# Moving the softmax sums of four heads behind one head's values, and the next rope in front of their reciprocal

## The chip, the cores and the metric

The kernel runs on one core of one Trainium2 chip. The core has a matrix engine (TensorE; in profiles PE for its products and PEld for the loading of the stationary operand), a vector engine (VectorE, DVE), a scalar engine (ScalarE, ACT), a general engine (GpSimd, POOL) and a queue engine (SyncE, SP) that issues most DMA transfers. Each engine works through its own instructions in order, and waits on semaphores for the others. Products land in PSUM, which is used here as eight banks of 128 x 512 float32; everything else is in SBUF. All data is float32, and PE carries out each float32 product as two products in the trace.

The metric is the time of one execution in microseconds of device time. The kernel before takes 1343.32 us (median of 10 runs, 1342.91 to 1344.06).

## The reference, cut to what matters

One transformer block in parallel form: `x + attention(layernorm(x)) + experts(layernorm(x))`, with 4 sequences of 512 tokens and 512 features. The part that the change touches is the attention with 16 heads:

```python
q = concatenate([q_C, rope(q_R)]); k = concatenate([k_C, rope(k_R)])   # 128 + 64 per head
scores = clip(q @ k.T, -80, 80);  scores = where(causal, scores, -inf)
weights = softmax(scores / sqrt(192))
out = (weights @ v).reshape(B, S, H * D_H) @ W_O.T
```

The softmax is computed without a maximum: the exponentials `pt` are multiplied with the values first, and the result of each head is divided by the sums of its exponentials later.

## The kernel before, in words

The first half of the program (to about 655 us) is layernorm, routing and the experts, with pieces of attention's preparation mixed in. The second half is attention, in a loop (L1678 on) over `n` = 32 pairs of heads (4 sequences x 8 pairs), `i` = 0 to 31. Two pairs make a group `q` of four heads. The groups share one row-sum product, one reciprocal, one division and one output projection.

Nearly every instruction is wrapped in `keep(...)`, which pins it to the order in which the Python code names it. So the order of calls in the loop is the order of each engine's queue. For one pair `i` it is:

1. `scores(i)`: PE makes the scores of both heads, transposed, into six PSUM banks: `a0`, `a1` (first key block of each head), `b0`, `b1` (second and fourth block), `c` (third block of the first head) and `sd_i` (third block of the second head). The last one is not a bank of its own but one from the pool `ps_p`, tag `pj`, which has three buffers and hands them out in turn.
2. `rotary_query(i + 1)` and `query(i + 1, 0)`: PE makes the rotary part `pqr` and the first head's query `pq_0` of the next pair, each into a `pj` buffer.
3. `weights(i)`: DVE clips the six banks into `pt_i` in the order `a0`, `a1`, `sd`, `c`, `b0`, `b1` (line 1457), ACT takes exponentials (L1461), POOL multiplies the diagonal blocks with a triangle (L1465) and then adds the four key blocks of each head into a 128 x 512 tile `su_i_j` (L1489 and L1493). The rope of the next pair's query, `turn_q`, is five DVE products (L1266 and L1269) and a POOL subtraction (L1270). On odd `i` it stands right behind the clips on DVE and in front of the `su` additions on POOL; on even `i` it is named after the sums, and so stands behind the reciprocal on DVE and behind the `su` additions on POOL.
4. On even `i` from 2 on: `sums(q)` with `q = i // 2 - 1`. PE adds the 128 partitions of four tiles `su` (those of pairs `i-2` and `i-1`) with a 128 x 32 block of ones, four products that fill the four 32-partition strips of one tile `sb` in bank `a0` (L1528). DVE takes the reciprocal `rc` (L1530). `spread_by_dma` issues 16 DMAs on SP that copy each strip of `rc` four times into a tile `rb` of 128 partitions (L1540).
5. `values(i - 1, 0)`: PE multiplies `pt` of the last pair's first head with the values, four products into a `pj` buffer `av` (L1509); ACT copies it to `og` (L1519).
6. `query(i + 1, 1)`, then on some pairs preparation for the next sequence, then `values(i - 1, 1)`.
7. On even `i` from 4 on `project_out(q - 1)`: the output projection of the group before, 56 products of 128 x 256 in PE's records, with DVE and POOL additions into `acc`. On odd `i` from 3 on `divide(q)`: DVE multiplies the four heads in `og` with `rb` (L1560) and forms factors for the projection (L1566, L1569).

So the three `pj` buffers are taken, in one pair of the steady loop, by `sd`, `pqr`, `pq_0`, `av_0`, `pq_1`, `av_1`, in that order: `av_0` follows `sd` in its buffer, and may be written only when DVE has clipped `sd`. In the same way `sb` may be written only when DVE has clipped bank `a0`, and the next pair's scores may be written into `a0` only when DVE has read `sb` for the reciprocal. There are 15 groups whose sums run in the loop (`i` = 2, 4, ... 30); the last group's stand after it.

Of the kernel before, what the change touches and what calls it, by code (L numbers as in the profile page):

```python
# [42 lines left out]
def kernel(  # L43
# [1166 lines left out]
    def lat(b, i):  # L1210
        return xnT[:, i, ts(b, S)]
# [40 lines left out]
    def turn_keys(b, psum=None):  # L1252
        if psum is None:
            dst, src = (lat(b, i).rearrange("p (k f) -> p k f", k=TPB) for i in (3, 1))
            for step in turn4(dst, src):
                step()
            return
        tp = psum(f"ckvt_{b}")
        for k in range(TPB):
            keep(nc.tensor.transpose(tp[:, ts(k, P)], lat(b, 1)[:, ts(k, P)], ident))  # L1260
        keep(nc.scalar.copy(lat(b, 3), tp))
# [16 lines left out]
    def rotary_query(i, ps):  # L1278
        b, hp = pairs[i]
        keep(nc.tensor.matmul(ps, qrT[:, hp, :], lat(b, 0), start=True, stop=True))  # L1280
        raw = hw.tile([P, S], F32, tag="raw", name=f"qraw_{i}")
        qr = hw.tile([P, S], F32, tag="qr", name=f"qr_{i}", bufs=1)
        qs[i] = [qr]

        def copy():
            keep(nc.scalar.copy(raw, ps))

        def turn():
            rope(qr, raw, f"q{i}")

        return copy, turn

    def query(i, j, ps):
        b, hp = pairs[i]
        keep(nc.tensor.matmul(ps, a_h[:, 2 * hp + j, :], lat(b, 0), start=True, stop=True))  # L1295
        qc = hw.tile([P, S], F32, tag=f"qc{j}", name=f"qc_{i}_{j}", bufs=1)
        qs[i].append(qc)

        def copy():
            keep(nc.scalar.copy(qc, ps))  # L1300

        return copy
# [99 lines left out]
    def psum(name):  # L1402
        return ps_p.tile([P, S], F32, tag="pj", name=name)
# [6 lines left out]
    def scores(i):  # L1410
        b = pairs[i][0]
        qr, *qc = qs.pop(i)
        bank = {}
        for j in range(2):
            bank[j, 0] = ps_s.tile([P, S], F32, tag=f"a{j}", name=f"sa_{i}_{j}")
            bank[j, 1] = bank[j, 3] = ps_s.tile([P, S], F32, tag=f"b{j}", name=f"sb_{i}_{j}")
        bank[0, 2] = ps_s.tile([P, S], F32, tag="c", name=f"sc_{i}")
        bank[1, 2] = psum(f"sd_{i}")

        def where(j, kc):  # L1420
            o = 3 * P if kc == 3 else 0
            return bank[j, kc][:, o : o + PT_W[kc]]

        order = [(j, kc) for kc in (0, 2, 1, 3) for j in range(2)]
        for j, kc in order:

            keep(
                nc.tensor.matmul(  # L1428
                    where(j, kc),
                    lat(b, 1)[:, ts(kc, P)],  # L1430
                    qc[j][:, kc * P :],
                    start=(kc != 3),
                    stop=False,
                )
            )
        for j, kc in order:
            r = slice(j * DHR, (j + 1) * DHR)
            keep(
                nc.tensor.matmul(  # L1439
                    where(j, kc),  # L1440
                    lat(b, 2)[r, ts(kc, P)],
                    qr[r, kc * P :],
                    start=False,
                    stop=(kc != 1),
                )
            )
        return bank

    def weights(i, bank, then, behind):

        pt = ap.tile([P, 5 * S], F32, tag="pt", name=f"pt_{i}")

        def clip(to, src):
            keep(nc.vector.tensor_scalar(to, src, CLIP, -CLIP, ALU.min, ALU.max))  # L1457

        def exp(t):

            keep(nc.scalar.activation(t, t, AF.Exp, scale=QK_SCALE))  # L1461

        def mask(t, at, k=1, step=P):
            m = t[:, at : at + P]
            keep(nc.gpsimd.tensor_mul(m, m, tri))  # L1465

        for j in range(2):
            a = pt[:, ts(j, S)]
            clip(a, bank[j, 0])
            exp(a)  # L1470
            mask(pt, PT[j, 0])
        half = 2 * P
        for j in (1, 0):
            clip(pt[:, PT[j, 2] : PT[j, 2] + half], bank[j, 2][:, :half])
        exp(pt[:, ts(2, S)])
        for j in range(2):
            mask(pt, PT[j, 2])
        then()
        for j in range(2):
            t = pt[:, ts(3 + j, S)]  # L1480
            clip(t, bank[j, 1])
            exp(t)
            mask(pt, PT[j, 1])
            mask(pt, PT[j, 3])
        behind()
        su = []
        for j in range(2):
            t = ap.tile([P, S], F32, tag="su", name=f"su_{i}_{j}", bufs=4)
            keep(nc.gpsimd.tensor_copy(t[:, :P], pt[:, PT[j, 0] : PT[j, 0] + P]))  # L1489
            for kc in range(1, TPB):  # L1490
                prev = pt[:, PT[j, 0] + P : PT[j, 0] + S] if kc == 1 else t[:, kc * P :]
                keep(
                    nc.gpsimd.tensor_add(  # L1493
                        t[:, kc * P :], prev, pt[:, PT[j, kc] : PT[j, kc] + PT_W[kc]]
                    )
                )
            su.append(t)
        pts[i], sus[i] = pt, su
# [3 lines left out]
    def values(i, j):  # L1502

        b, q = pairs[i][0], i // 2
        pt = pts[i]
        av = psum(f"av_{i}_{j}")
        for kc in range(TPB):
            keep(
                nc.tensor.matmul(  # L1509
                    av[:, kc * P :],  # L1510
                    lat(b, 3)[:, ts(kc, P)],
                    pt[:, PT[j, kc] : PT[j, kc] + PT_W[kc]],
                    start=(kc == 0),
                    stop=(kc == TPB - 1),
                )
            )
        if q not in og:
            og[q] = ap.tile([P, 4, S], F32, tag="og", name=f"og_{q}")
        keep(nc.scalar.copy(og[q][:, 2 * (i % 2) + j, :], av))  # L1519

    def bank(tag):
        return lambda name: ps_s.tile([P, S], F32, tag=tag, name=name)

    def sums(q):

        sb = bank("a0")(f"sb_{q}")
        for j, su in enumerate(sus.pop(2 * q) + sus.pop(2 * q + 1)):
            keep(nc.tensor.matmul(sb[ts(j, 32), :], ones[:, :32], su, start=True, stop=True))  # L1528
        rc = ap.tile([P, S], F32, tag="rc", name=f"rc_{q}", bufs=1)
        keep(nc.vector.reciprocal(rc, sb))  # L1530
        return rc
# [3 lines left out]
    def spread_by_dma(q, rc):  # L1535
        spread[q] = []
        for j in range(4):
            rb = ap.tile([P, S], F32, tag="rb", name=f"rb_{q}_{j}", bufs=4)
            for m in range(4):
                nc.sync.dma_start(rb[ts(m, 32), :], rc[ts(j, 32), :])  # L1540
            spread[q].append(rb)
# [123 lines left out]
    def combine(g):  # L1665
        for k, yg in enumerate(picks.pop(g)):
            keep(
                nc.vector.scalar_tensor_tensor(  # L1668
                    acc[:, g, :], yg, wk[:, g, k : k + 1], acc[:, g, :], ALU.mult, ALU.add
                )  # L1670
            )
# [6 lines left out]
    for i in range(n):  # L1678
        more = i + 1 < n
        even = i % 2 == 0  # L1680
        q = i // 2 - 1
        held = scores(i)
        raw_copy, turn_q = rotary_query(i + 1, psum(f"pqr_{i + 1}")) if more else (nothing, nothing)
        qc_copy = query(i + 1, 0, psum(f"pq_{i + 1}_0")) if more else nothing
        weights(i, held, raw_copy, nothing if even else turn_q)
        qc_copy()
        if even and i > 0:
            spread_by_dma(q, sums(q))
        if even:
            turn_q()  # L1690
        if i > 0:
            values(i - 1, 0)
        if more:
            query(i + 1, 1, psum(f"pq_{i + 1}_1"))()
        if i < 2:
            project(2 + i, psum)
        if 1 < i < 5:
            turn_keys((2, 3, 1)[i - 2], psum)
        if i > 0:
            values(i - 1, 1)  # L1700
        if even and i > 2:
            project_out(q - 1, first_added=lambda: combine(q))
        if i == 1:
            combine(0)
        if even and i != 2 or i == 1:
            fetch((i + 1) // 2)
        if not even and i > 1:
            divide(q)

    q = n // 2 - 1  # L1710
# [60 lines left out]
```

## Time and profile before

| What | Value |
|---|---|
| median of 10 runs | 1343.32 us |
| the profiled execution: its own time | 1343.4 us |
| its span, from first to last instruction | 1341.6 us |
| granted TensorE clock, mean | 0.999 |
| PE products busy | 1329.7 us (99%) |
| DVE busy | 967.3 us (72%) |
| POOL busy | 851.6 us (63%) |
| ACT busy | 406.0 us (30%) |
| DMA queue 1 | 34.0% of 16 engines |

The page gives each engine's busy time over the whole span. A row of the timeline has a start and a length in us, then the engine, the line, the operation, what it writes and reads, the shape and how many instructions were merged into the row; in brackets stands how long the engine had been idle before it and what ended that. "issue" means that nothing in the profile ended it. PE's products are pipelined: a row's start is firm, its end is modelled, and the time that a product occupies PE is read from the distance of starts. Over the 32 pairs a group of two pairs takes about 41.3 us (the first weights of `sb` of two neighbouring groups start at 860.09 and 901.38).

### The profile page before, as it was taken

The numbers are of one execution on the slowest core, as the hardware profiler recorded it, in microseconds if no ns is written. First come the engines' busy times: TensorE is split into PE (matmuls) and PEld (weight loads), VectorE is DVE, ScalarE is ACT, GpSimd is POOL, SyncE is SP. The second block draws the span as 40 slices with busy tenths as digits, with TensorE's granted clock in tenths as the row PEclk, the third lists the DMA queues.
The fourth block names the chain that finished last, engine by engine and source line by source line (L and its number), as shares of the span: only waits on it lengthen the run. The fifth ranks groups of instructions, "written<-read, shape, count | busy, mean of one in ns | idle before, by whom it ended". The sixth has DMA issues, their size and how long they took to land.

```text
span 1341.6 us, 17908 instructions
## 1 busy us (share of the span) xinstructions
PE 1329.7 (99%) x5949; PEld 993.1 (74%) x5949; DVE 967.3 (72%) x1414; ACT 406.0 (30%) x714; POOL 851.6 (63%) x956
## 2 busy tenths in 40 slices
PE   9999999999999999999999999999999999999997
PEld 8778888888888888877655766666666666666675
DVE  7669486666766676676458678877789777798774
ACT  3333222322223322222224333332323323243231
POOL 5113664554545465532267889888898888888883
PEclk9999999999999999999999999999999999999999
DMA  7850356766667675522401331243321333313342
GB/s 276 193 160 20 92 133 159 220 187 175 196 166 199 170 218 162 169 86 92 152 21 36 110 110 53 74 125 110 110 81 55 117 110 110 105 35 121 102 121 76
DMA packets 174101, 167.90 MB, mean 125 GB/s; under 512 B 57905, under 2 KB 136753, under 8 KB 174001
## 3 DMA queue, kind: packets, MB, share of 16 engines
q1 hardware_dynamic: 161264, 133.10, 34.0%
q0 software_dynamic: 12736, 33.57, 8.5%
q8 instruction: 49, 0.80, 0.2%
q14 instruction: 52, 0.42, 0.1%
HBM read 116.02 MB, written 34.87 MB: 112 GB/s over the span
## 4 chain that ended last, share of the span: by engine, by line
PE 98%; DVE 1%; ACT 0%; issue 0%; POOL 0%; DVEq 0%; ACTq 0%; POOLq 0%
PE op L228 14%; PE hr L228 11%; PE yr L228 11%; PE av L1509 11%; PE gr L228 10%; PE sb L1428 4%; PE sa L1428 4%; PE pq L1295 4%; PE gs L228 3%; PE sa L1439 3%; PE ys L228 2%; PE pqr L1280 2%; PE hs L228 2%; PE sb L1439 2%; PE sb L1528 2%; PE h_s L142 1%
## 5 line engine op out<-in xcount | busy, mean ns | idle before, releaser
L180 POOL DMA_INDIRECT xs<-xn_d,idx_i x208 | 229.0, 1101 | 195.0 <-DVE xT L197 136.0
L1465 POOL TENSOR_TENSOR pt<-pt,tri 128x128 f32<-128x128 f32 x256 | 139.6, 566 | 69.1 <-ACT pt L1461 62.3
L1461 ACT ACTIVATE pt<-pt 128x512 f32<-128x512 f32 x160 | 94.4, 628 | 258.1 <-DVE pt L1457 257.1
L1509 PEld LDWEIGHTS av<-pt,xnT 128*128 128x128 f32 x512 | 95.4, 190 | 83.7 <-issue 47.7
L1509 PE MATMUL av<-pt,xnT 128*128 128x512 f32 (+3 forms) x512 | 149.8, 436 | 0.0
L228 PE MATMUL op<-m,og 128*128 128x256 f32 x512 | 118.8, 380 | 0.8 <-DVE og L1560 0.8
L1269 DVE TENSOR_TENSOR swap_q<-qraw,sinT 32x512 f32<-32x512 f32 x128 | 117.7, 919 | 1.7
L1493 POOL TENSOR_TENSOR su<-su,pt 128x256 f32<-128x256 f32 (+1 forms) x128 | 105.2, 822 | 10.0
L228 PEld LDWEIGHTS op<-m,og 128*128 128x128 f32 x512 | 95.9, 190 | 15.0 <-DVE og L1560 1.9
L1457 DVE TENSOR_SCALAR pt<-sa 128x512 f32<-128x512 f32 x64 | 41.0, 682 | 75.2 <-PE sa L1439 75.2
L1603 POOL TENSOR_TENSOR acc<-acc,v 128x512 f32<-128x512 f32 x64 | 85.6, 1339 | 14.4 <-DVE acc L1606 8.5
L1655 POOL DMA_INDIRECT yg<-y_d,pos_i x48 | 54.5, 1135 | 56.6 <-issue 50.0
L228 PE MATMUL op<-m,s 128*128 128x256 f32 x384 | 88.1, 379 | 0.0
L1493 POOL TENSOR_TENSOR su<-pt 128x384 f32<-128x384 f32 x64 | 83.8, 1310 | 0.0
L228 PEld LDWEIGHTS op<-m,s 128*128 128x128 f32 x384 | 73.0, 190 | 9.9
L1606 DVE TENSOR_TENSOR acc<-op,acc 128x512 f32<-128x512 f32 x48 | 31.7, 686 | 54.9 <-POOL acc L1603 47.3
L1668 DVE SCALAR_TENSOR_TENSOR acc<-yg,wk,acc 128x512 f32<-128x512 f32 x48 | 56.7, 1181 | 19.1 <-POOL acc L1603 17.9
L1599 ACT COPY v<-op 128x512 f32<-128x512 f32 x64 | 37.5, 585 | 108.4 <-PE op L228 107.2
L1560 DVE TENSOR_TENSOR og<-og,rb 128x512 f32<-128x512 f32 x64 | 68.2, 1126 | 0.6 <-PE rb L1548 0.2
L228 PE MATMUL yr<-w,at_r 128*128 128x256 f32 x288 | 66.9, 380 | 0.3
L228 PE MATMUL hr<-xT,w 128*128 128x256 f32 x288 | 66.1, 379 | 0.0
L228 PE MATMUL gr<-xT,w 128*128 128x256 f32 x288 | 66.1, 379 | 0.0
(337 smaller groups left out, 2805.3 us busy)
## 6 DMA issues: line engine op xcount, KB each, us to landing
m<-m_d SPq DMA_DIRECT2D x112, 256.0 KB, 5.7
w<-in_L_ffn_W_dram SPq DMA_DIRECT2D x52, 512.0 KB, 4.4
rb<-rc SPq DMA_DIRECT2D x240, 64.0 KB, 2.0
w<-in_L_ffn_Wg_dram SPq DMA_DIRECT2D x26, 512.0 KB, 3.5
y_d<-v_yr SPq DMA_DIRECT2D x36, 256.0 KB, 2.2
y_d<-none SPq DMA_DIRECT2D x24, 256.0 KB, 4.7
acc<-in_L_attn_x_dram SPq DMA_DIRECT2D x16, 256.0 KB, 4.7
xn_d<-xp SPq DMA_DIRECT2D x16, 256.0 KB, 2.4
```

The costliest lines, as they stand in the source:

```text
L180: nc.gpsimd.indirect_dma_start(out=xs[blk][:, q, :], out_offset=None, in_=xn_d[:, :], in_offset=bass.IndirectOffsetOnAxis(ap=idx_i[:, q, b ...
L228: nc.tensor.matmul(banks[k][:, t, :], a[p][:, j, ts(t, P)], b[p][:, j, :], start=(k not in used), stop=(t == j == 1), skip_group_check=True,)
L1269: keep(nc.vector.tensor_mul(swap[there, :], raw[here, :], tables[1][here, :]))
L1428: nc.tensor.matmul(where(j, kc), lat(b, 1)[:, ts(kc, P)], qc[j][:, kc * P :], start=(kc != 3), stop=False,)
L1439: nc.tensor.matmul(where(j, kc), lat(b, 2)[r, ts(kc, P)], qr[r, kc * P :], start=False, stop=(kc != 1),)
L1461: keep(nc.scalar.activation(t, t, AF.Exp, scale=QK_SCALE))
L1465: keep(nc.gpsimd.tensor_mul(m, m, tri))
L1493: nc.gpsimd.tensor_add(t[:, kc * P :], prev, pt[:, PT[j, kc] : PT[j, kc] + PT_W[kc]])
L1509: nc.tensor.matmul(av[:, kc * P :], lat(b, 3)[:, ts(kc, P)], pt[:, PT[j, kc] : PT[j, kc] + PT_W[kc]], start=(kc == 0), stop=(kc == TPB - 1),)
L1560: keep(nc.vector.tensor_mul(o[:, j, :], o[:, j, :], rb))
L1603: keep(nc.gpsimd.tensor_add(block, block, v))
L1668: nc.vector.scalar_tensor_tensor(acc[:, g, :], yg, wk[:, g, k : k + 1], acc[:, g, :], ALU.mult, ALU.add)
```

## The change

In the loop over pairs, the block `if even and i > 0: spread_by_dma(q, sums(q))` moves down by two statements: behind `turn_q()` and behind `values(i - 1, 0)`.

```diff
         weights(i, held, raw_copy, nothing if even else turn_q)
         qc_copy()
-        if even and i > 0:
-            spread_by_dma(q, sums(q))
         if even:
             turn_q()
         if i > 0:
             values(i - 1, 0)
+        if even and i > 0:
+            spread_by_dma(q, sums(q))
         if more:
             query(i + 1, 1, psum(f"pq_{i + 1}_1"))()
```

On PE the four products of `sb` then stand behind the four of `av_0` and in front of `pq_1`. On DVE the reciprocal stands behind the five products of the rope instead of in front of them. On SP the 16 DMAs of `rb` keep their place between the same neighbours. ACT and POOL keep their orders. No instruction is added or left out.

## The prediction

> **What bounds the kernel now.** I read the page's busy times first, then the chain that ended last, then the waits of the attention half, then two even pairs instruction by instruction.
>
> ```profile
> PE 1329.7 (99%) x5949; PEld 993.1 (74%) x5949; DVE 967.3 (72%) x1414; ACT 406.0 (30%) x714; POOL 851.6 (63%) x956
> ...
> PE 98%; DVE 1%; ACT 0%; issue 0%; POOL 0%; DVEq 0%; ACTq 0%; POOLq 0%
> ```
>
> PE is the bound: its chain is 98% of the span. A change pays or costs what it does to PE's stream, and idle DVE or POOL time is worth nothing by itself. A modelled 99% hides short stops, so I looked at what the weight loads waited for:
>
> ```profile
> PEld av L1509 <- DVE pt L1457: 15.3, 29, 0.8
> ...
> PEld sb L1528 <- DVE pt L1457: 11.4, 15, 0.8
> ...
> PEld sb L1528 <- POOL su L1493: 4.4, 13, 0.4
> ```
>
> (Total us, times, longest.) In 13 of the 15 groups PE stops inside the sums for POOL's last `su` addition. And the first `av` product of a pair is released by a clip of DVE. Now the typical group `q` = 5, even pair `i` = 12, first PE's weight loads, then DVE, then POOL:
>
> ```profile
> 900.44 0.19 PEld L1295 LDWEIGHTS pq<-xnT,a_h 128*128 128x128 f32 x1 [0.24 <-issue]
> 901.38 0.15 PEld L1528 LDWEIGHTS sb<-su,ones 128*32 128x32 f32 x6 [0.76 <-DVE pt L1457]
> 901.88 0.14 PEld L1528 LDWEIGHTS sb<-su,ones 128*32 128x32 f32 x2 [0.34 <-POOL su L1493]
> 902.85 0.30 PEld L1509 LDWEIGHTS av<-pt,xnT 128*128 128x128 f32 x2 [0.84 <-DVE pt L1457]
> ```
>
> ```profile
> 899.22 1.48 DVE L1569 TENSOR_TENSOR og<-og 128x512 f32<-128x512 f32 x1
> 900.63 1.28 DVE L1457 TENSOR_SCALAR pt<-sa 128x512 f32<-128x512 f32 x2
> 901.83 0.41 DVE L1457 TENSOR_SCALAR pt<-sd 128x256 f32<-128x256 f32 x1
> 902.16 0.41 DVE L1457 TENSOR_SCALAR pt<-sc 128x256 f32<-128x256 f32 x1
> 902.49 1.27 DVE L1457 TENSOR_SCALAR pt<-sb 128x512 f32<-128x512 f32 x2
> 903.68 3.34 DVE L1530 RECIPROCAL rc<-sb 128x512 f32<-128x512 f32 x1
> 906.95 0.80 DVE L1266 TENSOR_TENSOR qr<-qraw,cosT 128x512 f32<-128x512 f32 x1
> 907.76 4.08 DVE L1269 TENSOR_TENSOR swap_q<-qraw,sinT 32x512 f32<-32x512 f32 x4
> ```
>
> ```profile
> 900.23 1.59 POOL L1493 TENSOR_TENSOR su<-su,pt 128x256 f32<-128x256 f32 x2
> ```
>
> `pq_0` starts at 900.43 and gives PE free at 901.29 (two products, 0.43 apart). `sb`'s weights go in at 901.38, but those of the second pair's `su` only at 901.88, 0.06 after POOL's addition ends at 901.82. DVE comes late out of the last odd pair's `divide`: it starts the clips only at 900.63, ends `a0` at about 901.30 and `sd` at 902.24. Today the clip of `sd` hides behind `sb`.
>
> **The change part by part.**
>
> *The wait for `su`, removed.* By the chain, `sb` takes 1.47 us and `av_0` 2.35 here, 3.82 together. At `q` = 0, where `su` was long ready, they take 1.00 + 2.35 = 3.35. So the wait is worth 0.47 a group. After the change `sb` starts over 2 us later than `su` ends, so it's gone: 13 x 0.47 = 6.1 us gained, if nothing takes its place.
>
> *The new neighbours of `sb`.* `sb` uses a quarter of the array's columns at a time, and PE stops in front of and behind it: weights at 901.38 instead of at the product before, and `av` takes 2.35 behind `sb` against 2.16 behind `pq`. After the change the stops stand between `av` and `sb` and between `sb` and `pq`. The trace has such a pair of edges in the last group: two `av` take 4.31 (2 x 2.16), then `sb` 0.99 by the chain, and its 0.1 behind `sb` falls on the projection. So I keep 3.35 for both blocks in either order, cost 0, bounds -0.1 to +0.1 a group.
>
> *The new wait: `av_0` for the clip of `sd`.* `av_0` takes over `sd`'s `pj` buffer, the fourth of three buffers in turn, so its first weights wait for that clip. Without a wait they go in one product ahead: on an odd pair `pq` ends at 846.16 and the weights of `av` go in at 845.73. Now they go in at 902.24 + 0.06 = 902.30, and the product holds PE 0.1 longer since its load hides behind nothing (902.86 to the next `pq` at 905.12 is 2.26, against 846.16 to 848.32). The stop is 902.30 + 0.10 - 901.29 = 1.11 us. The block then takes 3.35 + 1.11 = 4.46 instead of 3.82: **+0.64 us a group**. The other groups from `q` = 2 on have the same distances within 0.02, with one sum: where DVE is 0.1 later (`q` = 4), `su` is too. Group 1 has no `su` wait: `pq_0` is over at 736.13, the clip of `sd` ends at 736.62, so the stop is 736.68 + 0.10 - 736.13 = 0.65, less 0.02 that `sb` loses today: +0.63. Group 0 has DVE early (clip of `sd` over at 705.14, `pq_0` at 706.54): 0. Sum: 13 x 0.64 + 0.63 = 8.9, say **+8.9 us**. This already contains the gain above.
>
> Behind the waiting weight load stand all of PE's later products, so `sb`, `pq_1`, `av_1` and the projection move with it. Nobody makes it up: DVE's clips on odd pairs wait for PE (4.04 us idle at 884.51), so DVE's lateness starts anew from PE's scores each group, and its 16 us of unbroken work to the next even clip stay as they are.
>
> *The rope ahead of the reciprocal on DVE.* Its copy `qraw` is there in time (ACT, about 903.7). It takes 4.92 between starts beside POOL's additions (906.95 to 911.87) and 4.48 on odd pairs beside the masks (887.63 to 892.11). The reciprocal then starts at about 908.2 to 908.6, long after `sb`, and ends near the same 911.9. From `i` = 4 on that costs 0: bank `a0` is wanted again only after the projection (920), and the first DVE addition of the projection keeps its place. At `i` = 2 there is no projection:
>
> ```profile
> 705.39 1.27 DVE L1457 TENSOR_SCALAR pt<-sb 128x512 f32<-128x512 f32 x2
> ...
> 707.84 3.36 DVE L1530 RECIPROCAL rc<-sb 128x512 f32<-128x512 f32 x1 [1.18 <-PE sb L1528]
> ```
>
> ```profile
> 713.23 0.30 PEld L1428 LDWEIGHTS sa<-qc,xnT 128*128 128x128 f32 x2
> ```
>
> Pair 3's scores go into `a0` at 713.23. After the change the rope runs from 706.7, the reciprocal from 711.2 (711.6 with the slow rope) to 714.5 (715.0). The scores wait until 714.6 and start cold: between +1.3 and +1.8 us, once. I take **+1.4**, nearer the fast rope, since POOL is in its masks then.
>
> *SP.* The 16 DMAs of `rb` go out some 5 us later (from about 912 instead of 907.05, for 10 us). `divide` wants them at 933 or so (892.11 for the group before), and the `m` loads behind them in the queue (917.18, 3.56 us) slide to 922, wanted at the next projection near 949. 0, and if that cover were gone, 5 us a group at most.
>
> *POOL.* Its masks lose DVE's reciprocal as an easy neighbour (0.45 us each beside it, 0.9 beside the rope), and its additions gain it. I expect it to end within 1 us of today, both ways. What counts is when its additions let DVE finish the projection: DVE is done at 921.88, and the scores want those banks at 922.59. That slack of 0.7 becomes 1.3 as PE comes 0.64 later, so 0.
>
> A rule to weigh: in this case the granted clock stays at 0.999 although PE already stops 0.8 us around each `sb`, so by this row stops of 1.1 us cost only themselves. The Trainium skill, page "TensorE: Matmul & The Clock Gate", section "A second HAM failure mode: psum-queue depth-cycling", warns that short stops between groups can let the clock fall to half. If each of 15 stops cost one window of 3.4 us at half speed, an estimate from that page is 26 us more; the trace speaks against it.
>
> **Sum.** 8.9 + 1.4 = 10.3 us on the profiled 1343.4, so 1353.7; the profiled execution is 0.1 above the median, which gives **1353.6 us**. The main case's own range is 14 groups at 0.54 to 0.74 (the bounds of `sb`'s edges) plus 1.3 to 1.8: 1352.2 to 1355.5.
>
> **The rivals.**
>
> *Faster: the `sd` clip doesn't hold `av_0`* (DVE out of `divide` 1.1 us earlier, or the buffer free). For it: POOL's new rhythm might shorten DVE's products, which vary from 0.69 to 1.76 us by POOL's company. Against it: `divide` runs in the odd pair, where nothing is moved. Then 1343.3 - 6.1 + 1.4 = 1338.6. It decides at 0.47 us of stop: with less the group gains. Chance 0.07.
>
> *About the same: half of it.* DVE is early by 0.5 to 0.7 us, the stop shrinks to about the removed wait, and only `i` = 2 is paid: 1344.7. Chance 0.04.
>
> *Slower still: POOL slides past its slack.* If the masks beside the rope set POOL back by 2 us instead of under 1, the `sb` scores wait for DVE's last addition, 0.7 a group more: 1353.6 + 13 x 0.7 = 1362.7. For it: POOL is nearly full (8 tenths). Against it: it gets the reciprocal's 3.3 us back in its additions. Chance 0.09.
>
> **How the numbers follow.** Main case 0.80. Differences within 0.2% (2.7 us) can't be told from none. Slower 0.80 + 0.09 = 0.89; same 0.04; faster 0.07. For the range I leave out the faster and equal cases (0.11) and half of POOL's, and widen the main range by a stop that is 0.1 smaller or 0.3 larger per group: 1350.5 to 1359.0.
>
> **What would show it.** Right: `PEld av <- DVE pt` has about 1.4 to 1.6 us of idle in front of it at 14 places; `PEld sb <- POOL su` is gone; one wait of a scores load for the reciprocal of about 1.3 us near 714; reciprocals start right behind the rope without a wait. Wrong: `av` weights that go in right at `pq_0`'s end, a total below 1346, or new waits of the `sb` scores for DVE additions. What I can't see from before is POOL's length beside the moved rope; that's the step I trust least.

## The result, and the profile after

| | median us | range | runs |
|---|---|---|---|
| before | 1343.3 | 1342.78 to 1344.06 | 28 |
| after | 1353.47 | 1352.92 to 1354.62 | 8 |

The ratio after to before is 1.0076, with a 95% interval of 1.0068 to 1.0085: the change costs 10.2 us. The predicted time was 1353.6 us. The profiled execution after took 1353.91 us, with a span of 1352.1 us and a granted clock of 0.999.

The page of the kernel after, its busy times and the engines' shares of the chain that ended last:

```profile
PE 1327.9 (98%) x5949; PEld 992.9 (73%) x5949; DVE 959.5 (71%) x1414; ACT 404.9 (30%) x714; POOL 855.5 (63%) x956
...
PE 77%; DVE 16%; issue 3%; DMA 1%; SPq 1%; ACT 1%; DVEq 0%; POOL 0%; ACTq 0%; POOLq 0%
```

PE has the same 5949 products, and its busy time is even 1.8 us shorter. But its share of the chain fell from 98% to 77%, and DVE has 16%. That doesn't mean that 16% of the time is lost to DVE. The chain is followed back from each stop to what released it, and then along that engine's own earlier work. One stop is enough to lead it through 11 us of DVE's work (at `q` = 5 from 895.50 to 906.51). What the change costs is the stops themselves, the time by which PE's next product starts late, and the view of waits in the attention half of the kernel after has them (total us, times, longest):

```profile
PEld av L1509 <- DVE pt L1457: 26.6, 30, 1.8
...
PE av L1509 <- DVE pt L1457: 11.2, 14, 0.9
...
PEld sa L1428 <- DVE rc L1530: 1.2, 1, 1.2
```

The first row was 15.3 us before. The second is new: 14 times, PE itself stood still until a clip was done. The third is the one wait at `i` = 2. The waits of `sb` for POOL's `su` (4.4 us, 13 times) and for DVE's clips (11.4 us, 15 times) are both gone.

The typical group, `q` = 5, in the timeline of the kernel after: the weight loads, then DVE.

```profile
904.71 0.19 PEld L1295 LDWEIGHTS pq<-xnT,a_h 128*128 128x128 f32 x1 [0.24 <-issue]
906.55 0.30 PEld L1509 LDWEIGHTS av<-pt,xnT 128*128 128x128 f32 x2 [1.65 <-DVE pt L1457]
...
908.90 0.16 PEld L1528 LDWEIGHTS sb<-su,ones 128*32 128x32 f32 x8
909.90 0.30 PEld L1295 LDWEIGHTS pq<-xnT,a_h 128*128 128x128 f32 x2 [0.84 <-ACT qc L1300]
```

```profile
903.49 1.48 DVE L1569 TENSOR_TENSOR og<-og 128x512 f32<-128x512 f32 x1
904.89 1.27 DVE L1457 TENSOR_SCALAR pt<-sa 128x512 f32<-128x512 f32 x2
906.09 0.41 DVE L1457 TENSOR_SCALAR pt<-sd 128x256 f32<-128x256 f32 x1
...
912.48 3.36 DVE L1530 RECIPROCAL rc<-sb 128x512 f32<-128x512 f32 x1
```

The clip of `sd` ends at 906.09 + 0.41 = 906.50, and the first weights of `av_0` go in at 906.55. `sb` follows without any wait, and its neighbour `pq_1` has the same 0.84 in front of it that `av_0` had before. The reciprocal stands at the end of DVE's row of work and waits for nothing.

To compare kernels below I use two lengths. A **block** runs from the start of `pq_0`'s last product to the start of `pq_1`'s second product; it holds `sb` and `av_0` in either order, and without any stop it is 4.21 us (0.43 + 3.35 + 0.43). **Attention** runs from the start of the first scores product to the start of the last product of the kernel. A single length is good to 0.01 us, a sum of 15 blocks to some hundredths.

| | block at `q` = 0, 1, from 2 on | sum of the 15 blocks | attention |
|---|---|---|---|
| before | 4.21, 4.23, 4.67 | 69.29 | 677.37 |
| after | 4.21, 4.85, 5.30 | 78.04 | 687.40 |
| difference | 0, 0.62, 0.63 | 8.75 | 10.03 |

At `q` = 4 DVE is 0.1 us later in both kernels, and the block is longer in both: 4.78 before and 5.41 after, a difference of 0.63 as well. So the blocks carry 8.75 us, and 10.03 - 8.75 = 1.28 us lie elsewhere in attention. That is the new wait at `i` = 2, in the timelines of DVE and of the weight loads after:

```profile
711.60 3.36 DVE L1530 RECIPROCAL rc<-sb 128x512 f32<-128x512 f32 x1
```

```profile
715.01 0.30 PEld L1428 LDWEIGHTS sa<-qc,xnT 128*128 128x128 f32 x2 [1.22 <-DVE rc L1530]
```

Nothing else in attention changed length by more than hundredths.

### The profile page after: what moved, and what is told of

It reads as the page before. It is cut to its first block, busy times and chain, and to the rows that moved or that the text cites. A ratio compares the mean times of both kernels' runs of the same rounds, so it can differ in the third digit from the quotient of the medians.

```text
span 1352.1 us, 17908 instructions
## 1 busy us (share of the span) xinstructions
PE 1327.9 (98%) x5949; PEld 992.9 (73%) x5949; DVE 959.5 (71%) x1414; ACT 404.9 (30%) x714; POOL 855.5 (63%) x956
## 4 chain that ended last, share of the span: by engine, by line
PE 77%; DVE 16%; issue 3%; DMA 1%; SPq 1%; ACT 1%; DVEq 0%; POOL 0%; ACTq 0%; POOLq 0%
PE op L228 13%; PE hr L228 11%; PE yr L228 11%; PE gr L228 10%; PE av L1509 5%; DVE og L1560 5%; DVE pt L1457 4%; PE gs L228 3%; PE ys L228 2%; PE hs L228 2%; PE sa L1428 2%; PE sb L1428 2%; DVE s L1569 2%; DVE swap_q L1269 1%; DVE og L1569 1%
## 5 line engine op out<-in xcount | busy, mean ns | idle before, releaser
L1465 POOL TENSOR_TENSOR pt<-pt,tri 128x128 f32<-128x128 f32 x256 | 164.0, 660 | 75.7 <-ACT pt L1461 69.0
L1269 DVE TENSOR_TENSOR swap_q<-qraw,sinT 32x512 f32<-32x512 f32 x128 | 108.0, 844 | 1.7
L1493 POOL TENSOR_TENSOR su<-su,pt 128x256 f32<-128x256 f32 (+1 forms) x128 | 90.6, 708 | 10.0
L1493 POOL TENSOR_TENSOR su<-pt 128x384 f32<-128x384 f32 x64 | 77.1, 1205 | 0.0
L1295 PE MATMUL pq<-xnT,a_h 128*128 128x512 f32 x128 | 66.6, 605 | 0.0
L1668 DVE SCALAR_TENSOR_TENSOR acc<-yg,wk,acc 128x512 f32<-128x512 f32 x48 | 53.8, 1122 | 17.6 <-POOL acc L1603 16.4
```

The source lines that it names most:

```text
L1269: keep(nc.vector.tensor_mul(swap[there, :], raw[here, :], tables[1][here, :]))
L1493: nc.gpsimd.tensor_add(t[:, kc * P :], prev, pt[:, PT[j, kc] : PT[j, kc] + PT_W[kc]])
```

## The experiments

My theory: two waits are exchanged on PE. The wait of `sb` for POOL's last `su` addition (0.47 us a group) goes, and a longer one of `av_0` for DVE's clip of `sd` comes (1.1 us), because both have `pq_0`'s end as their start and `av_0` wants `sd`'s buffer. DVE's part of the change costs only one wait at `i` = 2. Rivals: DVE's new order costs something in each group (through POOL or the projection); the new place of `sb` on PE costs by itself; DVE's late clips have nothing to do with it.

Four kernels (`dve_only`, `pe_only`, `sd_first`, `after_thin_divide`) ran on a chip on which the kernel before itself took 1371.21 us (1363.73 to 1380.09). The extra time lay ahead of attention: the first scores started at 675.9 to 688.2 us instead of 657. For these I compare the length of attention; three of them were run again elsewhere.

### One half of the change at a time

`dve_only` puts the reciprocal behind the rope on DVE, and leaves `sb` ahead of `av_0` on PE.

```diff
-    def sums(q):
+    def sums(q, between=lambda: None):
         ... # the four products of sb
+        between()
         ... # the reciprocal
@@
-        if even and i > 0:
-            spread_by_dma(q, sums(q))
-        if even:
+        if even and i > 0:
+            spread_by_dma(q, sums(q, turn_q))
+        elif even:
             turn_q()
         if i > 0:
             values(i - 1, 0)
```

> Only the vector engine's part of the change: the four sum products stay where the kernel before has them on PE, and the reciprocal goes behind the next pair's rope. Theory 1 (the clip of sd holds av_0; the moved reciprocal costs only where no projection follows, at i = 2): PE's blocks of sb and av_0 stay at 3.82 us, one wait of the next scores for the reciprocal near 714 us, total before + 1.3 = 1344.6 us. Theory 2 (the cost comes from sb's stops between other neighbours on PE): also before + 1.3, it does not tell these two apart. Theory 3 (the late reciprocal, or POOL beside the moved rope, costs 0.6 us in every group): 1343.3 + 8.7 + 1.3 = 1353.3 us.

> The same kernel as dve_only (only the reciprocal goes behind the rope), on a chip where the spread is small enough for 1.3 us. Theory 1: before + 1.3 = 1344.6 us, all of it in one wait at i = 2. Theory 3 (the late reciprocal costs in each group): 1353 us.

`pe_only` moves the products of `sb` behind `av_0`, and leaves the reciprocal ahead of the rope.

```diff
-        if even and i > 0:
-            spread_by_dma(q, sums(q))
-        if even:
-            turn_q()
         if i > 0:
             values(i - 1, 0)
+        if even and i > 0:
+            spread_by_dma(q, sums(q))
+        if even:
+            turn_q()
```

> Only PE's part of the change: the four sum products go behind av_0, the reciprocal stays in front of the rope on DVE. Theory 1: av_0's weights wait for the clip of sd as in the changed kernel, 14 groups x 0.62 = +8.7 us. The reciprocal then waits some 2 us for sb, and the rope ends 2 us later; at i = 2 the rope (to 718 us) and POOL's subtraction come too late for pair 3's rotary scores, which want them at 717.75: +1.6 us there. In the other groups the late rope moves POOL by 1.3 us at its end, just at the limit of the slack of the projection's banks, 0 to 0.7 us a group. Total 1353.6 us, up to 1358. Theory 2: 1343.3 + 8.7 = 1352 to 1353.6, the same. Theory 3 (reciprocal behind the rope is what costs): about 1343.3 less the 6.1 us of the removed su wait = 1337 to 1339.

> The same kernel as pe_only (only the sum products go behind av_0). The first profile shows its attention part as long as the changed kernel's (687.5 and 687.4 us from the first scores product to the last product), so: 1353.5 us, within 1 us. Theory 3: 1337 to 1339 us.

| | median us (range) | ratio to before in the same session | block, from `q` = 2 on | sum of blocks | attention |
|---|---|---|---|---|---|
| `dve_only` | 1371.01 (1362.69 to 1382.85) | 1.0009 [0.9977, 1.0041] | 4.68 | 69.38 | 678.73 |
| `dve_only_again` | 1344.18 (1344.01 to 1345.34) | 1.0010 [1.0001, 1.0019] | 4.67 | 69.29 | 678.65 |
| `pe_only` | 1379.0 (1374.83 to 1385.76) | 1.0060 [1.0034, 1.0086] | 5.30 | 78.12 | 687.50 |
| `pe_only_again` | 1353.29 (1352.98 to 1353.66) | 1.0076 [1.0060, 1.0092] | 5.30 | 78.06 | 687.43 |

Attention agrees within 0.1 us between the two chips, which is why I trust that measure. DVE's half costs 678.65 - 677.37 = 1.28 us and leaves every block as it was. PE's half costs what the whole change costs. So the new order of DVE is not what slows the groups; the place of `sb` on PE is.

The halves add up to more than the whole, 1.28 + 10.06 against 10.03, and `i` = 2 shows why. In `pe_only_again` the reciprocal holds DVE instead, since it stands in front of the rope and must wait for the later `sb`. The timelines of DVE, POOL and the weight loads:

```profile
709.51 3.36 DVE L1530 RECIPROCAL rc<-sb 128x512 f32<-128x512 f32 x1 [3.33 <-PE sb L1528]
```

```profile
717.26 1.26 POOL L1270 TENSOR_TENSOR qr<-qr,swap_q 128x512 f32<-128x512 f32 x1 [2.02 <-DVE swap_q L1269]
```

```profile
718.57 0.30 PEld L1439 LDWEIGHTS sa<-qr,xnT 64*128 64x128 f32 x4 [1.26 <-POOL qr L1270]
```

DVE stands still for 3.33 us, the rope comes late, POOL's subtraction comes late, and the rotary scores of pair 3 wait. That costs 1.13 us there (from `sa`'s first to its rotary weights 5.65 instead of 4.52), most of the 1.3 us that `pe_only_again` loses outside its blocks (10.06 less 8.77). The change as made avoids this by the rope in front, and pays 1.28 for `a0` instead. So each half alone pays about 1.3 us at `i` = 2, and both together pay it once. `pe_only` makes DVE wait for `sb` in every group (32.6 us at 15 places in all), and only at `i` = 2 does that cost PE anything.

### Is it the clip of `sd`, and is it DVE's lateness?

`sd_first` is the kernel after with one thing moved: on even `i` from 4 on DVE clips `sd` before `a0` and `a1`.

```diff
+        half = 2 * P
+        early = i % 2 == 0 and i > 2
+        if early:
+            clip(pt[:, PT[1, 2] : PT[1, 2] + half], bank[1, 2][:, :half])
         ... # the clips of a0 and a1
-        half = 2 * P
-        for j in (1, 0):
+        for j in (0,) if early else (1, 0):
```

> The changed kernel, with the clip of sd moved to the first place among DVE's six clips on even pairs from 4 on. Theory 1: the clip of sd is over 1.2 us earlier (about 0.18 us after pq_0's last product starts instead of 1.37), av_0's weights go in 0.24 us after it instead of 1.42, the block from pq_0 to pq_1 falls from 5.30 to 4.2 to 4.3 us at 14 places, and the total is 1343.3 - 13 x 0.42 + 1.3 = 1339.2 us, below the kernel before. Theory 2 (sb's stops between av_0 and pq_1 cost the time): unchanged, 1353.5 us. Theory 3: unchanged or worse, since a0 is clipped 0.4 us later and POOL's masks start later: 1353.5 us or more.

> The same kernel as sd_first. The first profile shows blocks of 4.21 us in all groups and an attention part 4.0 us shorter than before's, so: 1339.3 us, 1.5 us above the best version, which has no wait at i = 2. Theory 2: 1353.5 us.

Measured: 1364.46 us (1358.96 to 1380.2), ratio 0.9954 [0.9927, 0.9982] on the first chip, and 1339.56 us (1338.78 to 1339.78), ratio 0.9970 [0.9959, 0.9980] on the other, attention 673.39 and 673.40. All blocks are 4.21. DVE's clips and the weight loads of `sd_first_again` in the same group:

```profile
900.74 0.41 DVE L1457 TENSOR_SCALAR pt<-sd 128x256 f32<-128x256 f32 x1
901.08 1.27 DVE L1457 TENSOR_SCALAR pt<-sa 128x512 f32<-128x512 f32 x2
```

```profile
900.55 0.19 PEld L1295 LDWEIGHTS pq<-xnT,a_h 128*128 128x128 f32 x1 [0.24 <-issue]
901.21 0.39 PEld L1512 LDWEIGHTS av<-pt,xnT 128*128 128x128 f32 x2 [0.47 <-DVE pt L1457]
903.65 0.16 PEld L1531 LDWEIGHTS sb<-su,ones 128*32 128x32 f32 x8
904.65 0.30 PEld L1295 LDWEIGHTS pq<-xnT,a_h 128*128 128x128 f32 x2 [0.84 <-ACT pt L1461]
905.58 0.30 PEld L1512 LDWEIGHTS av<-pt,xnT 128*128 128x128 f32 x2 [0.63 <-ACT qc L1300]
```

The same order on PE and the same work on DVE are now faster than before. One clip, 1.2 us earlier, is worth 1353.47 - 1339.56 = 13.9 us, so the clip of `sd` is the cause of the loss. The last line shows what is late next: the second head's `av_1`, which takes over `pq_0`'s buffer, waits a little for ACT's copy `qc` out of it. It costs 0.06 us a group (from `pq_1`'s second product to the first weights of the next scores 14.52 instead of 14.46) and 0.17 at `q` = 4, some 0.9 in all. That is why attention is 14.0 us shorter than in the kernel after and not the 14.9 us of the blocks.

To see whether the moved clip is a gain by itself, `before_sd_first` has the same edit on the kernel before.

> The kernel before with the clip of sd first among DVE's clips on even pairs from 4 on, a control for the run of the changed kernel with that clip first. Theory 1: sb waits for the clip of a0, which is 0.33 us later (901.70 instead of 901.38), but its second half waits for POOL's su at 901.88 anyway; the blocks stay at 4.67 us and the total at 1343.3 us (within 1 us). If the clip's place by itself gave time: 1338 to 1340 us.

Measured: 1343.29 us (1342.68 to 1343.89), ratio 0.9999 [0.9990, 1.0009], blocks 4.22 and 4.67. Under the old order the clip of `sd` hides behind `sb`, as the prediction said. The timeline of its weight loads shows that `sb` now waits longer for `a0` (1.05 idle instead of 0.76). The wait for `su` has no row of its own any more, but it still ends last: the eight loads take 0.32 us instead of 0.16, because the last of them goes in 0.05 us after POOL's addition ends at 901.13. So the block ends where it ended before:

```profile
901.00 0.32 PEld L1531 LDWEIGHTS sb<-su,ones 128*32 128x32 f32 x8 [1.05 <-DVE pt L1457]
902.16 0.30 PEld L1512 LDWEIGHTS av<-pt,xnT 128*128 128x128 f32 x2 [0.84 <-issue]
```

The opposite test is `one_more_clip`: the kernel after, in which DVE clips bank `c` once more, ahead of all other clips, on even `i` from 4 on. It does 0.33 us of DVE work twice.

```diff
+        if i % 2 == 0 and i > 2:
+            clip(pt[:, PT[0, 2] : PT[0, 2] + 2 * P], bank[0, 2][:, : 2 * P])
         ... # the clips in their order
```

> The changed kernel with one more DVE instruction on even pairs from 4 on: the clip of c (128 x 256, 0.33 us from start to start) is done once more, ahead of the other clips. A dose of DVE lateness and of nothing else. Theory 1 (av_0 waits for the clip of sd, and DVE has no slack up to there): each of 14 groups 0.33 us longer, av_0's weights 1.75 us after pq_0's last product starts instead of 1.42, blocks of 5.63 instead of 5.30: 1353.5 + 4.6 = 1358.1 us. If PE's stop has another cause than the place of sd's clip in DVE's queue: 1353.5 us.

Measured: 1357.93 us (1357.48 to 1358.33), ratio 1.0109 [1.0092, 1.0125]. DVE, then the weight loads:

```profile
905.98 0.41 DVE L1457 TENSOR_SCALAR pt<-sc 128x256 f32<-128x256 f32 x1
906.31 1.27 DVE L1457 TENSOR_SCALAR pt<-sa 128x512 f32<-128x512 f32 x2
907.51 0.41 DVE L1457 TENSOR_SCALAR pt<-sd 128x256 f32<-128x256 f32 x1
```

```profile
907.97 0.30 PEld L1511 LDWEIGHTS av<-pt,xnT 128*128 128x128 f32 x2 [1.97 <-DVE pt L1457]
```

The block grows from 5.30 to 5.63, by 0.33, which is just the distance of starts of the added clip. Fourteen of them make 4.62 us (82.66 - 78.04), and attention grows by 4.63. DVE's time ahead of that clip goes one for one into the kernel's time.

`after_thin_divide` asks why DVE is late at all. It is the kernel after with the division of odd pairs on 8 of 512 columns.

```diff
-            keep(nc.vector.tensor_mul(o[:, j, :], o[:, j, :], rb))
+            keep(nc.vector.tensor_mul(o[:, j, :8], o[:, j, :8], rb[:, :8]))
```

> The changed kernel with most of the division left out: the four products of L1560 work on 8 of 512 columns (their waits stay, the result is not the softmax's). It takes some 3.5 to 4 us from DVE's unbroken work between an odd pair's scores and the next even pair's clips. Theory 1 (DVE's lateness out of divide is the cause): the clip of sd is over before pq_0 ends, no stop of av_0 in any group, PE's block is 4.21 us everywhere; 1343.3 - 6.2 + 1.3 = 1338.4 us. Theory 2: PE's order is as in the changed kernel, and so is its time: 1353 us. Theory 3: 1353 us less what POOL gains from a quieter DVE.

`before_thin_divide` has the same edit on the kernel before.

> The kernel before with most of the division left out (the four products of L1560 on 8 of 512 columns; the result is not the softmax's). Theory 1: POOL's additions lose DVE's company in the odd pair and start earlier, su is ready in time and the 0.47 us stop inside sb goes in 13 groups: 1343.3 - 6.2 = 1337.1 us, 1.3 us below the changed kernel with the same left out, which is then all that the change costs. If su's lateness has nothing to do with divide: 1343.3 us.

| | median us (range) | ratio to before in the same session | sum of blocks | attention |
|---|---|---|---|---|
| `after_thin_divide` | 1364.7 (1359.74 to 1370.54) | 0.9966 [0.9940, 0.9992] | 63.1 | 671.77 |
| `before_thin_divide` | 1336.18 (1335.94 to 1336.91) | 0.9947 [0.9932, 0.9963] | 63.1 | 670.52 |

With DVE early, both orders have blocks of 4.21 throughout, and the two kernels differ in attention by 671.77 - 670.52 = 1.25 us, the price of `i` = 2. So `sb` behind or in front of `av_0` is the same to PE when nothing is late. The waits of both kernels, the one for POOL's `su` and the one for the clip of `sd`, go when most of the division in the odd pair is left out. `before_thin_divide` gains 0.9 us more than its expectation; 0.7 of it lies at the end, where the last group's division is waited for (from the last `sb` to the start of the last product 19.73 instead of 20.42).

### Taking the buffer away, and the best of both

`swap_banks` leaves the clips in their order and exchanges the banks: from `i` = 6 on `av_0` goes into `a0`, which DVE clips first, and `sb` into the `pj` buffer of `sd`. At `i` = 2 and 4 it keeps the old order.

```diff
-        av = psum(f"av_{i}_{j}")
+        swap = j == 0 and i % 2 == 1 and 4 < i < n - 1
+        av = (bank("a0") if swap else psum)(f"av_{i}_{j}")
@@
-        sb = bank("a0")(f"sb_{q}")
+        swap = 1 < q < n // 2 - 1
+        sb = (psum if swap else bank("a0"))(f"sb_{q}")
@@
+        if i in (2, 4):
+            spread_by_dma(q, sums(q))
         if even:
             turn_q()
         if i > 0:
             values(i - 1, 0)
-        if even and i > 0:
+        if even and i > 4:
             spread_by_dma(q, sums(q))
```

> The sums behind av_0 and the reciprocal behind the rope from i = 6 on (old order at i = 2 and 4), and the two PSUM buffers exchanged: av_0 of those pairs goes into bank a0, sb into the pj buffer that sd has left. Theory 1: av_0 then waits for the clip of a0, 0.94 us earlier than that of sd: weights at about 0.49 us after pq_0's last product starts, stop 0.17 us, block 4.38 us instead of 5.30 (before: 4.67) in 13 groups, and no cost at i = 2: 1343.3 - 13 x 0.3 = 1339.4 us. Theory 2 (order on PE costs): 1343.3 + 13 x 0.6 = 1351 us.

Measured: 1339.44 us (1338.97 to 1340.46), ratio 0.9971 [0.9961, 0.9981], block 4.38, attention 673.49. DVE's first clips and the weight loads of `q` = 5:

```profile
900.42 1.28 DVE L1457 TENSOR_SCALAR pt<-sa 128x512 f32<-128x512 f32 x2
```

```profile
901.15 0.30 PEld L1510 LDWEIGHTS av<-pt,xnT 128*128 128x128 f32 x2 [0.72 <-DVE pt L1457]
```

`av_0` now waits for the first half of DVE's row `pt<-sa` instead of the clip after it, and 0.17 us of stop are left. No clip was moved here. So it's the buffer that `av_0` inherits that ties PE to the clip, not the values or the exponentials.

`best` joins what the runs showed: `sd`'s clip first, `sb` behind `av_0` from `i` = 4 on, and the old order at `i` = 2, where no projection covers the reciprocal.

```diff
+        if i == 2:
+            spread_by_dma(q, sums(q))
         if even:
             turn_q()
         if i > 0:
             values(i - 1, 0)
-        if even and i > 0:
+        if even and i > 2:
             spread_by_dma(q, sums(q))
```

(with the clip order of `sd_first`)

> The order of the change from i = 4 on only, the old order at i = 2, and the clip of sd first on even pairs from 4 on. Theory 1: no stop of su, next to none of sd, none of the reciprocal at i = 2: 1343.3 - 13 x 0.42 = 1337.8 us, the fastest of all. Theory 2 or 3: 1352 us.

Measured: 1337.76 us (1337.68 to 1338.04), ratio 0.9959 [0.9945, 0.9973]; all blocks 4.21, attention 672.14. It is 5.5 us faster than before and 15.7 faster than after. Its page, the same two lines as above:

```profile
PE 1324.0 (99%) x5949; PEld 991.3 (74%) x5949; DVE 953.5 (71%) x1414; ACT 402.2 (30%) x714; POOL 857.2 (64%) x956
...
PE 98%; DVE 1%; ACT 0%; issue 0%; POOL 0%; DVEq 0%; ACTq 0%; POOLq 0%
```

PE has the whole chain again, and the longest idle of `av`'s weights for a clip is 0.6 us, too short to stop PE.

## Why the prediction was right

*The removed wait (6.1 us gained).* Shown. No `sb` product waits for `su` in the kernel after, and with DVE early the blocks of the kernel before shrink from 4.67 to 4.21: 0.46 us a group against the 0.47 that was read.

*The new neighbours of `sb` (0).* Shown. The blocks are 4.21 in either order (after and before with the thin divide), and the sums of the blocks are both 63.1.

*`av_0` waits for `sd`'s clip (+0.64 a group, +0.63 at `q` = 1, 0 at `q` = 0).* Measured: +0.63, +0.62 and 0, in sum 8.75 where 8.9 was predicted. That the clip is what holds it was shown in three ways: the clip moved up takes the stop away, DVE lengthened by 0.33 lengthens the stop by 0.33, and another buffer for `av_0` takes 0.92 us of it away. The step said that DVE's lateness starts anew each group, so that nothing adds up and nothing is made up; the equal differences from `q` = 2 on and the equal rest (14.46 from `pq_1`'s second product to the first weights of the next scores in both kernels) agree. The rival in which DVE comes out of the division 0.5 to 0.7 us earlier did not occur: DVE's clips start 0.19 us after the second weights of `pq_0` before (900.63 and 900.44) and 0.18 after (904.89 and 904.71).

*`i` = 2 (+1.4, between 1.3 and 1.8).* Measured 1.28 at one place, named as such by the waits; a shade below the lower end. The rope between starts there took 711.60 - 707.19 = 4.41 us, the fast one of the two rows that I weighed.

*Rope and reciprocal from `i` = 4 on (0).* Shown by `dve_only_again`: all blocks as before, 1.28 us for `i` = 2 and nothing else. In the kernel after, the reciprocal starts 7.59 us after DVE's first clip; 7.6 to 8.0 were predicted.

*SP (0).* In the waits of the kernel after the division has only this one row. It belongs to the last group, whose reciprocal is spread by PE; no division waits for a DMA:

```profile
DVE og L1560 <- PE rb L1548: 0.2, 1, 0.2
```

*POOL (within 1 us, so 0).* This was the step that I trusted least. Six of its masks went from 2.70 to 4.33 us beside the rope; the `su` additions beside the reciprocal won it back. The timeline of POOL after:

```profile
907.57 4.33 POOL L1465 TENSOR_TENSOR pt<-pt,tri 128x128 f32<-128x128 f32 x6 [0.21 <-ACT pt L1461]
...
917.37 1.27 POOL L1270 TENSOR_TENSOR qr<-qr,swap_q 128x512 f32<-128x512 f32 x1
```

The subtraction starts 12.48 us after DVE's first clip, where it was 12.29 before: 0.19 us late. The rival that POOL would run out of its slack of 0.7 is thereby out, and PE's distance to the next scores shows no wait for it.

*The faster rival* said that the clip would not hold `av_0`, which would give 1338.6, and that it decides at 0.47 us of stop. The runs confirm that point from both sides without it being the case here: with a stop of 0.17 (`swap_banks`) or 0 (`sd_first_again`) the new order beats the old one. `sd_first_again` took 1339.56 and not 1338.6, because of the small wait of `av_1` for `qc` that I had not seen.

*The clock.* With 14 stops of about 1.1 us the granted clock stayed at 0.999. It was 0.998 with the 1.4 us stops of `one_more_clip`, as it was in `before_sd_first`, where PE stops no longer than in the kernel before. The Trainium skill, page "TensorE: Matmul & The Clock Gate", section "A second HAM failure mode: psum-queue depth-cycling", says that short idle times of PE between groups of products can make the clock swing between full and half speed; in attention no run here shows that.

*Small misses.* I gave the idle time ahead of `av`'s weights as 1.4 to 1.6 us; the rows show 1.65 and up to 1.8. It counts from the end of the load before, and so contains the 0.24 that a load idles anyway. The stated range, 1350.5 to 1359.0, is not quite the sum that it is said to be: 1352.2 less 14 times 0.1 is 1350.8, and 1355.5 plus 14 times 0.3 is 1359.7. The measured time lies inside by either. Both terms of the sum came out a little too high, 8.9 against 8.75 and 1.4 against 1.28; they did not make up for each other.

## What to carry to other kernels

When an instruction is moved up in the queue of the engine that is the bound, look up who used its output buffer last, and when that reader is done: a pool that hands out buffers in turn makes a wait that no line of the code names. Two waits that start at the same moment hide each other, and taking the shorter away is worth something only if the other isn't longer; here 0.47 went and 1.1 came, and clipping one tile earlier turned a loss of 10 us into a gain of 3.7 (5.5 with the old order kept at `i` = 2). Treat the first round of a loop on its own: what the projection covers in every later group stood bare at `i` = 2.

## What was not expected of the hardware

- In `av_0`'s rows the stop of PE can be read from the idle in front of its first weight load, less some 0.55 us: 1.65 went with a stop of 1.09, 1.97 with 1.42, 0.72 with 0.17, and 0.57 and 0.47 with none (idle from the timelines above and, for 0.57, one of `best`; stops as block less 4.21). So a wait of up to 0.57 cost at most 0.01 here: where nothing holds it, that load goes in one product ahead (at 845.73 in the kernel before, its product at 846.16). In front of `sb` and of the load behind it this does not hold: there 0.76 and 0.84 of idle stand in blocks of 4.21 too.
- On one chip the half of the program before attention was 19 to 31 us longer in the four kernels profiled there, at a granted clock of 0.97 to 1.00 in its stretches of 100 us, while attention was equal within 0.1 us in the three that were run again on another chip. What makes it longer stays open.
